# Routed experts in a two-layer decoder: whole rows in the experts' lists, outcomes in rows of their own, and first-layer weights loaded per tile

## The chip, the cores and the metric

The kernel runs on one core of a Trainium2 chip. A core has five engines that run their own instruction streams: TensorE (PE, with its weight loads shown as PEld), VectorE (DVE), ScalarE (ACT), GpSimd (POOL) and SyncE (SP). SP issues the plain DMAs; POOL issues the indirect ones, whose rows are given by a list of indices. The metric is the device time of one execution in microseconds. "Before" is the median of three runs, 733.93 us (733.42 to 735.83).

## The reference, cut to what matters

The reference is a decoder of two layers on x of 4 batches x 256 tokens x 256 channels, with a layer norm after each block. Layer 0 has a sliding-window attention, a cross attention over 1601 context rows and a feed-forward block with ternary weights. Layer 1 has a causal attention with compressed keys, a linear cross attention, and the block that the change is about, a mixture of eight experts of which each token uses two:

```python
logits = 30 * tanh(x @ w_gate / 30)           # x: 1024 tokens x 256
probs = softmax(logits)                       # over 8 experts
_, idx = top_k(probs, 2)
weights = probs * one_hot(idx, 8).sum(-2)
for e in range(8):
    h = silu(x @ w1[e]) * (x @ w3[e])         # 1024 x 512
    out = out + h @ w2[e] * weights[:, e:e+1]
x = layernorm(x + out)
```

All is computed in float32. The kernel computes each expert only for the tokens that chose it.

## The kernel before

**Order of the work.** The kernel's lines do not run in the order in which they stand. A planner, `Loom`, collects every operation with a duration, the tiles that it reads and writes and a priority, and `weave` then emits one at a time: the one that can start first by the planner's own clock, and among equals the one of lowest priority number. Each engine's order is thereby fixed when the program is built. `LAT` and `RATE` are the planner's constants for hops between engines and for DMA; `View` keeps which box of a tile an operation touches, from which the planner finds what depends on what. A `piece` is a group of PE instructions that are planned together.

**The stages.** For each batch of 256 tokens (two row tiles of 128, called t = 0 and t = 1): `l0_attention`, `l0_cross`, `l0_ffn`, `l1_attention`, `l1_cross`, `route`. `ternary` prepares the feed-forward weights of layer 0: it loads three matrices of 1 MB into `raw` (two buffers), sums their magnitudes on DVE, adds the sums over partitions by a small product on PE (`wabs` with `ones`), and loads the matrices again to round them. The stages of different batches overlap as the planner finds room.

**The experts before.** `route(b)` stores the batch's rows to two arrays in DRAM, `xd` (the rows to gather) and `acc` (to which outcomes are added). It computes the gates, each token's two experts and its place in each expert's list, and writes an entry of 8 bytes (gate, token number) into `lists` with four indirect DMAs. `tile_table` turns the counts into a table: for each expert tile of 128 list rows, which expert and which first row. It runs twice: once before the last batch is routed, for the tiles that are sure to be full (`EARLY`, 5), and once after (`LATE`, 18). There are 23 tiles in all, since a list's last tile is padded.

`expert_tile` does one tile. SP reads the first row from the table and fetches the tile's 128 entries; POOL gathers the tokens' rows from `xd` into `xg`; PE transposes them; PE multiplies with w1 and w3 of the expert, the tokens' rows being the stationary side and the weights, 512 wide, the moving one; ACT, DVE make the hidden layer `eh`, tokens on partitions; PE transposes it in four blocks, ACT copies it to `ehT`; PE multiplies with w2; DVE scales by the gate; POOL adds the outcome to `acc` with an indirect DMA that accumulates. The weights of all experts stand in SBUF: `w13` is loaded once layer 0 has freed its place, `w2e` once the even batches' attention buffers are free. The tiles' working buffers (`p6`) open when the last batch's `l1_attention` has ended, as they take its place.

At the end the four batches are loaded from `acc`, normalised and stored.

Of the kernel before, what the change touches and what calls it, by code (L numbers as in the profile page):

```python
# [23 lines left out]
F32 = mybir.dt.float32  # L24
# [22 lines left out]
class View:  # L47


    def __init__(self, buf, box, shape, steps=()):  # L50
        self.buf, self.box, self.shape, self.steps = buf, box, tuple(shape), steps

    def _with(self, name, args, kw, shape, box=None):
        return View(self.buf, box or self.box, shape, self.steps + ((name, args, kw),))

    def __getitem__(self, key):
        keys = key if isinstance(key, tuple) else (key,)
        keys += (slice(None),) * (len(self.shape) - len(keys))
        spans, shape = [], []
        for k, n in zip(keys, self.shape):  # L60
            if isinstance(k, slice):
                lo, hi, _ = k.indices(n)
                spans.append((lo, hi))
                shape.append(hi - lo)
            else:
                spans.append((k, k + 1))
        return self._with("__getitem__", (key,), {}, shape, None if self.steps else tuple(spans))
# [108 lines left out]
class Loom:  # L176
# [12 lines left out]
    RATE = 0.25  # L189
# [22 lines left out]
    def op(self, ways, outs, ins, claims=(), after=(), size=None, land=1.6, what="", unordered=False):  # L212
# [6 lines left out]
        for v in outs:  # L219
            b = v.buf  # L220
            if not unordered:
                op.deps.update(o for box, o in b.writes if meet(box, v.box))
            op.deps.update(o for box, o in b.reads if meet(box, v.box))
# [16 lines left out]
    def piece(self, us, claims=(), ins=(), what=""):  # L240
# [5 lines left out]
        self.op({"PE": (us, us, lambda: [f() for f in fns])}, outs, ins, claims, what=what)  # L246
# [54 lines left out]
    def weave(self):  # L301
# [11 lines left out]
        while left:  # L313
# [22 lines left out]
            if op.size is not None:  # L336
                self.free["DMA"] = max(self.free["DMA"], at + us) + op.size / self.RATE
                op.end, op.engine = self.free["DMA"] + op.land, "DMA"
# [70 lines left out]
def decoder(ctx: ExitStack, tc: tile.TileContext, a: dict, out: bass.AP):  # L409
# [23 lines left out]
    down = scope("left", [even], on=experts)  # L433
# [15 lines left out]
    p6w, p6d = experts.pool("p6w"), down.pool("p6d")  # L449
# [138 lines left out]
    def normalise(x):  # L588
        mv = tiny((P, 2, 2), "mv")
        for t in range(2):  # L590
            st = tiny((P, 6), "st")
            k.vector.bn_stats(st, x[:, t, :])
            k.vector.bn_aggr(mv[:, t, :], st)
        rstd = tiny((P, 2), "rstd")
        k.gpsimd.tensor_scalar(rstd, mv[:, :, 1], 1e-5, None, ALU.add)
        k.gpsimd.tensor_tensor(rstd, rstd, mhalf, ALU.pow)
        for t in range(2):
            k.vector.tensor_scalar(
                x[:, t, :], x[:, t, :], mv[:, t, 0:1], rstd[:, t : t + 1], ALU.subtract, ALU.mult
            )  # L600

    def norm(b, x):

        normalise(x)
        xt = xpool.tile((P, 2, S), F32, "xt")
        ps = bank((P, 2, 2, P))
        for t in range(2):
            with piece(0.22, [xt], what="norm"):
                for c in range(2):
                    turn(ps[:, c, t, :], x[:, t, c * P : (c + 1) * P], ident)  # L610
        evac(xt.rearrange("p c (t q) -> p c t q", t=2), ps)
        X[b], XT[b] = x, xt
# [12 lines left out]
    def project_out(pool, x_new, t, x_old, o, wo, gate=None):  # L625
# [8 lines left out]
        else:  # L634
            k.vector.scalar_tensor_tensor(oT, gate[:, :, t * P : (t + 1) * P], 1.0, pt, ALU.add, ALU.mult)
# [16 lines left out]
    def l0_attention(b):  # L652
# [11 lines left out]
        for i in range(3):  # L664
            pv = bank((P, D))
            with piece(0.86, what="v"):
# [67 lines left out]
    def feature_map(pool, dst, ps, n, width, bufs=2):  # L734

        e = pool.tile((P, 512), F32, "fm", bufs=bufs)[:n, :width]
        k.scalar.activation(e, ps, AF.Exp)
# [314 lines left out]
    def l1_attention(b):  # L1052
# [16 lines left out]
        def four(q4):  # L1069

            ps = project_in(XT[b], lambda c, j: m_w[:, c, 2 * q4 + j, :], [qeT], "q")
            evac(qeT[:, 2 * q4 : 2 * q4 + 2, :], ps)
            aT0 = pool.tile((P, 2, 2, S), F32, "aTa")
            aT1 = pool.tile((P, 2, 2, P), F32, "aTb")
            for t in range(2):
# [4 lines left out]
                with piece(0.65 if t == 0 else 1.15, [at, aT0, aT1], what="scores"):  # L1080
# [15 lines left out]
                for kc in range(t + 1):  # L1096
# [4 lines left out]
                    dst = aT0[:, :, :, t * P : (t + 1) * P] if kc == 0 else aT1  # L1101
                    evac(dst, pt.rearrange("p (u i) q -> p u i q", u=2))

            po = bank((P, 2, S))
# [452 lines left out]
```

## Time and profile before

| what | before |
|---|---|
| median of three runs | 733.93 us (733.42 to 735.83) |
| the profiled execution | 731.26 us |
| its span, first to last instruction | 729.5 us |
| mean granted TensorE clock | 0.979 |
| busy: PE, DVE, ACT, POOL | 92%, 60%, 41%, 22% |
| moved by DMA | 63.39 MB |

The span and all lines of the profile are of that one execution. A line number such as L253 can be that of a helper through which many operations go (L253 is every matmul, L260 every transpose, L382 every operation of DVE, ACT or POOL), so operations are told apart by the names of the tiles that they write and read. A matmul in float32 shows as two records. Matmuls are pipelined: the time from one start to the next tells what one costs, the duration of a record is longer.

### The profile page before, as it was taken

What the parts mean: (1) busy time and instruction counts of PE and PEld (TensorE: products, weight loads), DVE (VectorE), ACT (ScalarE), POOL (GpSimd) and SP (SyncE); (2) the same over time, 40 slices, a digit from 0 to 9 for tenths busy, and PEclk for the clock granted to TensorE, in tenths of its full rate; (3) what the DMA queues carried; (4) which work ended last, traced back from release to release, by engine and by line L of the source; (5) the groups of instructions that cost most, each with busy time, mean ns of one, the idle gap of its engine ahead of it and who ended that gap; (6) DMA issues with size and microseconds to landing.
All of it is one profiled execution on the core that took longest, in us unless ns stands there. A gap on an engine that the chain in (4) does not pass through costs nothing.

```text
span 729.5 us, 11204 instructions
## 1 busy us (share of the span) xinstructions
PE 672.8 (92%) x3920; PEld 490.8 (67%) x3920; DVE 438.5 (60%) x1067; ACT 302.6 (41%) x931; POOL 158.3 (22%) x190
## 2 busy tenths in 40 slices
PE   7999999999999999999899999999977959999970
PEld 5778787678867786767676777777654635665640
DVE  4899886334493535665999877887754513333323
ACT  2868664211232224343467765656611202222210
POOL 3220324022100000000121010303122456522232
PEclk9999999999999999999999999999999989999995
DMA  9901212538632230000203900003601143312214
GB/s 307 341 18 59 92 35 87 173 128 273 219 115 91 91 122 1 1 0 1 53 1 115 347 1 30 1 30 62 199 2 37 30 56 90 59 21 23 23 22 123
DMA packets 51819, 63.39 MB, mean 87 GB/s; under 512 B 7758, under 2 KB 41684, under 8 KB 51764
## 3 DMA queue, kind: packets, MB, share of 16 engines
q1 hardware_dynamic: 46836, 56.63, 23.9%
q0 software_dynamic: 4928, 6.05, 5.3%
q8 instruction: 32, 0.52, 0.3%
q14 instruction: 23, 0.19, 0.1%
HBM read 54.05 MB, written 8.61 MB: 86 GB/s over the span
## 4 chain that ended last, share of the span: by engine, by line
PE 73%; DVE 13%; DMA 5%; ACT 4%; issue 2%; POOL 1%; SPq 0%; POOLq 0%; DVEq 0%; ACTq 0%
PE bank L253 65%; PE bank L260 8%; DVE at L382 3%; ACT at L382 3%; DMA acc<-ey,mine 2%; DVE nm L382 2%; DVE x L382 2%; DVE h L382 1%; DVE as L382 1%; DMA lists<-entry,rowi 1%; DMA xg<-xd,mine 1%; DVE st L382 1%; DMA x<-acc 1%; POOL rstd L382 1%; DMA wqkv<-in_wqkvT 0%
## 5 line engine op out<-in xcount | busy, mean ns | idle before, releaser
L382 ACT ACTIVATE at<-at,nm 128x128 f32<-128x128 f32 (+1 forms) x256 | 106.3, 418 | 23.5 <-DVE nm L382 22.9
L253 PE MATMUL bank<-w,xgT 128*128 x184 | 85.0, 608 | 0.5 <-ACT xgT L382 0.5
L260 PE MATMUL bank<-ident,at 128*128 128x128 f32 (+1 forms) x440 | 60.4, 275 | 1.1 <-DVE at L382 0.4
L253 PEld LDWEIGHTS bank<-w,xgT 128*128 128x128 f32 x184 | 35.0, 197 | 37.1 <-issue 36.0
L260 PEld LDWEIGHTS bank<-ident,at 128*128 128x128 f32 (+1 forms) x440 | 50.7, 141 | 13.0 <-issue 4.8
L382 POOL TENSOR_SCALAR rstd<-mv 128x2 f32<-128x2 f32 x24 | 6.3, 263 | 244.2 <-DVE mv L382 226.1
L253 PE MATMUL bank<-V,aT 128*128 128x256 f32 (+1 forms) x240 | 55.2, 380 | 1.4 <-DVE o L382 1.4
L253 PE MATMUL bank<-KT,qT 128*128 128x512 f32 (+1 forms) x128 | 53.8, 554 | 0.0
L253 PEld LDWEIGHTS bank<-V,aT 128*128 128x128 f32 (+1 forms) x240 | 45.0, 190 | 11.6 <-issue 4.4
L1357 POOL DMA_INDIRECT acc<-ey,mine x23 | 36.1, 1569 | 72.7 <-DVE ey L382 42.1
L253 PE MATMUL bank<-kf,V 128*128 128x256 f32 (+1 forms) x208 | 49.9, 382 | 1.1 <-DVE kf L382 1.1
L382 DVE TENSOR_REDUCE nm<-at 128x4 f32<-128x512 f32 x64 | 50.7, 809 | 0.5
L253 PE MATMUL bank<-wkv,KT 128*128 128x256 f32 (+1 forms) x208 | 49.7, 383 | 0.0
L382 ACT ACTIVATION_READ_ACCUMULATOR at<-at,nm 128x1 f32 x256 | 48.4, 189 | 0.0
L253 PE MATMUL bank<-w2e,ehT 128*128 x184 | 43.9, 385 | 2.9 <-ACT ehT L382 2.8
L382 POOL TENSOR_TENSOR at<-at,rs 128x512 f32<-128x512 f32 (+1 forms) x17 | 20.3, 1191 | 111.0 <-DVE rs L382 70.0
L253 PEld LDWEIGHTS bank<-kf,V 128*128 128x128 f32 (+1 forms) x208 | 38.5, 190 | 7.7 <-DVE kf L382 2.3
L382 ACT COPY aT<-bank 128x512 f32<-128x512 f32 (+2 forms) x57 | 29.1, 540 | 33.3 <-PE bank L260 33.0
L253 PEld LDWEIGHTS bank<-wkv,KT 128*128 128x128 f32 (+1 forms) x208 | 37.7, 186 | 7.5 <-issue 1.9
L253 PEld LDWEIGHTS bank<-w2e,ehT 128*128 128x128 f32 x184 | 34.0, 190 | 12.3 <-ACT ehT L382 4.4
L382 DVE TENSOR_TENSOR at<-at,rs 128x512 f32<-128x512 f32 (+1 forms) x47 | 39.2, 834 | 1.0
L382 ACT ACTIVATE eh<-bank 128x512 f32<-128x512 f32 x23 | 13.7, 597 | 59.4 <-PE bank L253 59.4
(248 smaller groups left out, 1252.0 us busy)
## 6 DMA issues: line engine op xcount, KB each, us to landing
w<-in_w SPq DMA_DIRECT2D x16, 512.0 KB, 9.3
KT<-in_ctxT SPq DMA_DIRECT2D x6, 1024.0 KB, 6.2
V<-in_ctx SPq DMA_DIRECT2D x6, 1024.0 KB, 7.5
w2e<-in_w SPq DMA_DIRECT2D x8, 512.0 KB, 9.4
KT<-in_ctxT SPq DMA_DIRECT2D x6, 577.0 KB, 4.7
V<-in_ctx SPq DMA_DIRECT2D x6, 512.0 KB, 4.1
wq<-in_w1qT SPq DMA_DIRECT2D x8, 256.0 KB, 4.8
wo<-in_w1o SPq DMA_DIRECT2D x8, 256.0 KB, 3.1
```

The costliest lines, as they stand in the source:

```text
L253: lambda: self.nc.tensor.matmul(real(o), real(lhsT), real(rhs), start=real(start), stop=stop, **kw)
L260: fns.append(lambda: self.nc.tensor.transpose(real(o), real(x), real(ident)))
L382: return getattr(engine, method)(*[real(x) for x in args], **{k: real(x) for k, x in kw.items()})
L1357: nc.gpsimd.indirect_dma_start(out=acc.real(), out_offset=bass.IndirectOffsetOnAxis(ap=ids.real(), axis=0), in_=y.real(), in_offset=None, ...
```

## The change

**The lists.** An entry of `lists` becomes the token's whole row, its gate and the place of its outcome: 258 numbers, 1,032 bytes. `l1_cross` writes its result straight into the entry, `route` copies it to the entry of the token's second expert, and the arrays `xd` and `acc` go. `lists` is first filled with zeros (9216 rows, six DMAs).

**A tile.** The tile's table holds the row numbers, so POOL gathers the tile from `lists` in one indirect DMA, gate and place included; SP's fetch goes. The outcome is written, not added, to a row of its own in a new array `yd`: one for each token's first and one for its second expert, and spare rows for padding. Two such writes are declared to have no row in common.

**The products.** w1 and w3 become the stationary side, in blocks of 128 columns, and the tokens' rows the moving side, so that the hidden layer comes out with its channels on partitions; its transposes and their copy go. w1 and w3 are loaded by SP for each tile into one of four buffers `wt`, by the expert's number from the table, in place of `w13`. `w2e` is loaded where `w13` was.

**The last batch.** `l1_attention`, `l1_cross` and `route` of the last batch run in two halves (t = 0, t = 1). There are three tables: 5 tiles before the first half is routed, 2 before the second, 16 after it.

**The end.** Each batch loads two blocks from `yd` and adds them to its rows on DVE (eight loads, eight additions), then normalises and stores.

**The planner.** `RATE` goes from 0.25 to 0.33, indirect DMAs no longer queue behind others in its clock, `View` keeps boxes through chains of slices, and a `piece` can wait for the readers of a tile that its result will overwrite (`over`, used in `l0_attention` for v).

The diff, cut to its core:

```diff
-    RATE = 0.25
+    RATE = 0.33
...
-    down = scope("left", [even], on=experts)
...
-    p6w, p6d = experts.pool("p6w"), down.pool("p6d")
+    p6w = experts.pool("p6w")
...
-            with piece(0.86, what="v"):
+            with piece(0.86, over=[v], what="v"):
...
+        for ts in ((0,), (1,)) if b == B - 1 else ((0, 1),):
+            for q4 in range(4):
+                four(q4, ts)
...
+            norm_into(xn, xt, ts)
+            yield ts, xn, xt
...
-    EARLY = -(-(2 * 3 * S - NE * (P - 1)) // P)
-    LATE = 2 * T // P + NE - 1 - EARLY
+    EARLY = [-(-(2 * n - NE * (P - 1)) // P) for n in (3 * S, T - P)]
+    EARLY[1] -= EARLY[0]
+    TILES = 2 * T // P + NE - 1
+    LATE = TILES - sum(EARLY)
     LISTS = (NE + 1) * T
+    W = D + 2
...
-    lists = in_dram((LISTS, 2), "lists", I32)
-    xd = in_dram((T + P, D), "xd")
-    acc = in_dram((T + P, D), "acc")
+    lists = in_dram((LISTS, W), "lists")
+    yd = in_dram((2 * T + 1 + TILES * P, D), "yd")
...
+        blank = p3.tile((P, FF), F32, "h")[:, :W]
         k.gpsimd.memset(blank, 0.0)
+        for i in range(0, n, 12):
+            dst = lists[i * P : (i + 12) * P, :].rearrange("(n p) w -> p n w", p=P)
+            filled.append(k.dma_start(dst, blank.unsqueeze(1).to_broadcast([P, 12, W]), after=loaded))
...
+    def scatter(dst, row, src, us, land, what, after=(), level=None):
...
+            d = nc.gpsimd.indirect_dma_start(
+                out=dst.real(),
+                out_offset=bass.IndirectOffsetOnAxis(ap=row.real(), axis=0),
+                in_=src.real(),
+                in_offset=None,
+            )
+            tc.declare_no_dep(d.ins, group=what, reason="no two of them have a row in common")
...
-        for d in (xd, acc):
-            k.dma_start(d[b * S : (b + 1) * S, :].rearrange("(t p) d -> p t d", p=P), X[b])
...
+            x = entry[:, t, :, :D]
+            either(
+                (k.gpsimd, "tensor_copy", (x[:, 1], x[:, 0]), {}),
+                (k.vector, "tensor_copy", (x[:, 1], x[:, 0]), {}),
+                (k.scalar, "copy", (x[:, 1], x[:, 0]), {}),
+            )
...
-        def fetch():
-            first_row()
-            nc.sync.dma_start(out=entry.real(), in_=lists.real()[bass.ds(reg["row"], P), :])
...
-                in_=xd.real(),
-                in_offset=bass.IndirectOffsetOnAxis(ap=ids.real(), axis=0),
+                in_=lists.real(),
+                in_offset=bass.IndirectOffsetOnAxis(ap=rowi[:, i : i + 1].real(), axis=0),
...
-                compute_op=ALU.add,
...
+        def weights():
+            expert(nc.sync)
+            for j, w in enumerate(("w1", "w3")):
+                nc.sync.dma_start(
+                    out=wt.real()[:, j],
+                    in_=a[w][bass.ds(reg[nc.sync], 1), :, :].rearrange("o (c p) n -> p (o c) n", p=P),
+                )
...
+        wt = p6w.tile((P, 2, 2, EI), F32, "wt", bufs=4)
+        k.op({"SP": (1.6, 1.6, weights)}, [wt], [tab], size=8e-6 * D * EI, what="weights")
...
+        h = pool.tile((P, EI // P, P), F32, "eh")
+        pa = [bank((P, EI // P, P)), bank((P, EI // P, P))]
+        with piece(3.52, [h], what="tile"):
             for j in range(2):
+                for m in range(EI // P):
+                    for c in range(2):
+                        mm(pa[j][:, m], wt[:, j, c, m * P : (m + 1) * P], xgT[:, c, :], c == 0, c == 1)
...
-        hT = pool.tile((P, 4, P), F32, "ehT")
-        ph = bank((P, 4, P))
-        with piece(0.44, [hT], what="tile"):
-            for c in range(4):
-                turn(ph[:, c, :], h[:, c * P : (c + 1) * P], ident)
-        evac(hT, ph)
...
-        k.op({"POOL": (1.65, 1.65, add_up)}, [acc], [y, ids], size=0.13, what="add up")
+        scatter(yd, slots, y, 1.0, 2.0, "give")
...
-    w13 = p6w.tile((P, NE, 2, 2, EI), F32, "w13")
-    for e in range(NE):
-        k.dma_start(w13[:, e, 0], rows(a["w1"][e]))
-        k.dma_start(w13[:, e, 1], rows(a["w3"][e]))
-    w2 = p6d.tile((P, NE, 4, D), F32, "w2e")
+    w2 = p6w.tile((P, NE, 4, D), F32, "w2e")
...
     for b in range(B):
-        x = new_x()
-        k.dma_start(x, acc[b * S : (b + 1) * S, :].rearrange("(t p) d -> p t d", p=P))
+        x = X[b]
+        for e in range(2):
+            y = p6.tile((P, 2, D), F32, "back", bufs=4)
+            row0 = 1 + e * T + b * S
+            k.dma_start(y, yd[row0 : row0 + S, :].rearrange("(t p) d -> p t d", p=P))
+            k.vector.tensor_tensor(x, x, y, ALU.add)
         normalise(x)
```

## The prediction

> **What bounds the kernel now.** I read the page first: the share of each engine, the slices of the span and the chain of work that ended last.
>
> ```profile
> PE 672.8 (92%) x3920; PEld 490.8 (67%) x3920; DVE 438.5 (60%) x1067; ACT 302.6 (41%) x931; POOL 158.3 (22%) x190
> ...
> PE   7999999999999999999899999999977959999970
> ...
> PEclk9999999999999999999999999999999989999995
> ...
> PE 73%; DVE 13%; DMA 5%; ACT 4%; issue 2%; POOL 1%; SPq 0%; POOLq 0%; DVEq 0%; ACTq 0%
> ```
>
> PE is the bound nearly everywhere. It gives way in slices 29 to 31 (536 to 605 us), where the experts start, and in the last slice. Asked by windows, 536 to 605 holds 51.69 us of PE work in 69 and a clock of 0.90; 605 to 708 holds 101.10 in 103. So two things are worth money: PE work, and those holes. The timeline of PE shows both:
>
> ```profile
> 541.24 0.67 PE L260 MATMUL bank<-ident,x 128*128 128x128 f32 x4 [3.16 <-DVE x L382]
> ...
> 550.67 0.41 PE L260 MATMUL bank<-ident,xg 128*128 128x128 f32 x2 [2.80 <-DMA xg<-xd,mine]
> ...
> 596.45 0.66 PE L260 MATMUL bank<-ident,xg 128*128 128x128 f32 x2 [7.54 <-DMA xg<-xd,mine]
> ...
> 604.00 3.60 PE L253 MATMUL bank<-w,xgT 128*128 x8
> 607.44 0.60 PE L260 MATMUL bank<-ident,eh 128*128 128x128 f32 x4
> 607.87 3.60 PE L253 MATMUL bank<-w,xgT 128*128 x8
> ```
>
> Brackets are idle time and who ended it. All holes of 536 to 605 sum to 17.9 us (0.69, 3.16, 0.67, 2.80, 0.90, 0.35, 0.68, 7.54, 0.46, 0.66). Starts give prices: 8 records of w1/w3 take 3.44 us (0.43 each), four transposes of eh 0.44. A f32 matmul is two records. Why the gather that ends the 7.54 was late is in POOL's timeline:
>
> ```profile
> 583.49 0.96 POOL L1215 DMA_INDIRECT lists<-entry,rowi  x1 [0.30 <-issue]
> 584.75 1.59 POOL L1357 DMA_INDIRECT acc<-ey,mine  x1 [0.30 <-DVE eh L382]
> 591.48 1.56 POOL L1357 DMA_INDIRECT acc<-ey,mine  x1 [5.14 <-DMA acc<-ey,mine]
> 593.34 1.02 POOL L1349 DMA_INDIRECT xg<-xd,mine  x1 [0.31 <-issue]
> ```
>
> An add-up waits until the one before it has landed, and the gathers stand behind it in POOL's order. The end is the same wait, in the chain:
>
> ```profile
> 705.75 3.72 DMA acc<-ey,mine
> ...
> 710.20 3.73 DMA acc<-ey,mine
> ...
> 714.89 4.01 DMA x<-acc
> ```
>
> PE ends at 708.1 and the span at 729.5: a tail of 21.4 us.
>
> [...]four 128x128 records of wkv,gT start at 196.23 and the next group at 196.67, 0.11 each, as fast as transposes; so 128-wide products are no slower per column[...]. [...]after the 3.16 hole the 16 records of wqg take 5.29 us and not 3.72. [...]no run here shows gathers beside a load of weights, so their delay is bounded below. [...]the trace has 5.4 us for scatters of 8-byte entries against 2.8 for gathers of 1 KB rows.
>
> **The change, part by part.** 23 tiles in both kernels.
>
> *Hidden layer transposed by construction.* w1 and w3 become the stationary side, so eh needs no transposes: 92 x 0.109 = -10.0 us. Their products become 23 x 32 = 736 records at 0.112 = 82.4 us for 184 x 0.429 = 78.9: +3.5. Bounds: 0.109 (transposes), giving +1.3, and 0.13 (the 128x136 records of kvs,qf, 512.93 to 513.97), giving +17. I take 0.112, as wkv,gT is the same shape. ACT's copy of ehT (0.59 each) goes too, hidden but for the last ones.
>
> *One gather, no fetch.* The fetch (1.7 us to land, after SP's register loads) leaves the chain from routing to first product. Scatters now carry 1,032 B; bounds of landing 2.6 us (fastest gather) and 6.3 (the slowest 8-byte one of 536 to 545); I take 3.7, that of an add-up of 1 KB rows. From the rank products of batch 2: 1.25 us to the first scatter (533.4 to 534.65), four issues at 1.29, landing 3.7 after the fourth, 0.4, gather 3.0: first xg at +12.2. The changed PE order puts 11.7 us of other pieces in between (wqg, scores, pv, out, priced as above). Stall 0.5, range 0 to 4.
>
> *No wait between outcomes.* Rows of their own let outcomes be written without order. After the last rank products PE has w2 and w1/w3 of remaining early tiles, 12.7 us; two scatters and a gather need 10 to 12. The 7.54, 0.46 and 0.66 go.
>
> *Last batch in halves.* Expert buffers open only after its attention, so early tiles still cannot fill that, but two early tables and the cross half now fill the norms' waits: 3.16 and 2.80 are covered by w1/w3 of tiles 1 and 2 (3.6 each). New holes: the last head group's softmax (mask 1.4, max 1.2, exp 2.0, multiply 1.2, hops: 6.3) has 2.9 of cover, so 3.4; eviction of qeT 0.8; the first tile 0.5; the norm's rstd on POOL queues behind five gathers (6.3 us), PE waits for it about 1; small ones 1. Sum 7 left of 17.9: -10.9. Of the 4.7 us that the slow clock cost there (1.6 wqg, 1.1 and 1.5 w1/w3, 0.5 kvs) half goes: -2.3. The extra routing and table work of DVE (some 8 us) lies beside PE pieces; DVE is busy 26 of 69 there.
>
> *w1 and w3 per tile.* 24 MB through SP, one MB for each 5.5 us of PE, four buffers. The old load of w1/w3 ran at 385 GB/s (windows 400 to 415): 2.7 us per MB. Hidden; without that cover each us over 5.5 is paid per tile.
>
> *Filling the lists.* 9.5 MB in place of 2.4, queued on SP between the FFN weights' loads near 170 us. The old fill ran at 364 to 387 GB/s (windows 177.5 to 187.5): 25 to 30 us. The raw weight behind it lands near 210, its sum (2.3) is done near 213; PE meets the product of these sums near 218, by its order. Hidden with 5 us to spare; stores to xd and acc vanish.
>
> *The end.* ey, issue, landing: +4.2 us after PE (it was +5.8, two add-ups in a row), first load 2.7 later. DVE then has eight additions of 128x512 (0.6) beside the old work of 7.4: 12.4. Then 5.5 as before (724.0 to 729.5): 24.8 against 21.4, +3.4.
>
> *Planner.* RATE 0.33 and finer boxes re-order all stages; I expect nothing, within 3 us, since the early PE order differs only in interleaving.
>
> Sum: -10.0 + 3.5 - 10.9 - 2.3 + 3.4 = -16.3. The profiled execution was 731.26 (span 729.5), so 715.0 for its like; the median of runs is 733.93, 2.7 above it, so 717.6: say 717.5.
>
> **Rivals.** *The holes stay* (0.17): gathers beside 4 MB of weights land late, the first tile and the late tiles wait 5 us each: 727. [...]against: the order leaves 0.7 to 3 us of room. *The plan covers more* (0.12): the clock stays up, the softmax hole closes: 708. *The fill is late* (0.07): [...]PE waits 5: 722.5. *Slower* (0.09): the stream of weights becomes the bound. Each late tile then takes the load's time; it undoes the gain at 16.3 / 16 = 1.0 us more per tile, 6.5 us per MB or 160 GB/s. At 6.9 us: 717.6 + 22 = 740. For it: 512 KB took 9.3 us to land in the page's issues; against: that was the eighth in a queue moving 385 GB/s. That the change doesn't do what it says I give nothing: the transposes are gone from the order.
>
> **Numbers.** Likeliest 0.55: 717.5, own range 712 to 723. Faster: 0.55 + 0.17 + 0.12 + 0.07, less 0.03 for results near no change: 0.88. Within 0.3% (2.2 us, about what a measurement of this kernel can tell from no change): 0.03. Slower 0.09. Range 706 to 730: it leaves out the slower case and the outer parts of the second and third.
>
> **What would show it.** Right: no ident,eh; w1/w3 records 0.11 apart; PE idle under 8 us where 17.9 was; outcomes on POOL with no wait for one another; eight loads and 25 us after PE. Wrong: PE waiting for wt, for xg over 2 us, or for the sums of raw near 218; PE records of xgT,wt over 0.12 apart, which at 0.13 alone gives back 13 us.

## The result, and the profile after

The changed kernel takes 732.53 us (median of 20 runs, 726.92 to 734.21) where the kernel before, in the same comparison, takes 735.10 (median of 20, 732.07 to 738.22). The ratio is 0.9954, with a 95% interval of 0.9935 to 0.9973: half a per cent faster, clear of the noise, where 717.5 us had been forecast. The profiled execution took 726.92 us, its span is 725.2, its mean granted clock 0.971. Four of the 20 runs, the profiled one (the fastest) among them, show a clock of 0.971 or 0.973 and take 726.9 to 729.1 us, the other sixteen 0.966 or 0.967 and 731.7 to 734.2, so the profile shows less than the typical run loses.

The page of the changed kernel first: PE and its granted clock in 40 slices of 18.1 us, and the shares of the chain of work that ended last.

```profile
PE   7999999999999999999899899999988979979960
...
PEclk9999999999999999999999999999999989989995
...
PE 74%; DVE 9%; issue 5%; ACT 5%; POOL 3%; DMA 2%; another core or an unknown queue 1%; SPq 0%; POOLq 0%; DVEq 0%; ACTq 0%
```

PE works 669.5 us in all (672.8 before). The slices 30, 31 and 33, which had stood at 7, 7 and 5, have 8, 8 and 7: the holes are smaller. But slice 36, full before, has 7, and "issue" has grown from 2% to 5% of the chain: time in which the engine waited for nothing that the profile names. Of it, 4.4 us are PE's, near 592, and some 26 are POOL's, between 603 and 641. The timeline of PE shows the holes (start, duration, operation and count; the bracket is the idle time before it and what ended it, "remote" standing for something that the trace does not name):

```profile
406.88 2.79 PE L267 MATMUL bank<-ident,at 128*128 128x128 f32 x12 [2.47 <-ACT at L397]
...
537.58 0.41 PE L267 MATMUL bank<-ident,o 128*128 128x128 f32 x2 [2.66 <-DVE o L397]
...
551.08 0.41 PE L267 MATMUL bank<-ident,xg 128*128 128x128 f32 x2 [1.56 <-remote]
...
585.90 5.52 PE L260 MATMUL bank<-xgT,wt 128*128 128x128 f32 x48
592.14 0.27 PE L260 MATMUL bank<-xgT,wt 128*128 128x128 f32 x1 [0.72 <-issue]
...
598.53 2.28 PE L260 MATMUL bank<-xgT,wt 128*128 128x128 f32 x9 [0.34 <-issue]
600.61 2.17 PE L260 MATMUL bank<-w2e,eh 128*128 x8
...
642.39 0.82 PE L267 MATMUL bank<-ident,xg 128*128 128x128 f32 x6
647.70 3.78 PE L260 MATMUL bank<-w2e,eh 128*128 x8 [4.49 <-DVE eh L397]
```

The products of w1 and w3 are cheap where nothing disturbs them: the 48 records from 585.90 on start 0.112 apart, and no transpose of `eh` is left. There are three new losses. Near 405, in the first batch's `l1_attention`, PE waits 2.47 us for ACT's `at`; the kernel before has no such hole there. Between 591.3 and 598.5 the records that should follow each other at 0.11 come 0.7 or 1.4 us apart; the 64 records from 585.90 would have been issued by 593.1, and the next product starts at 600.61, 7.5 us late. And at 647.70 PE has waited 4.49 us for DVE's `eh`. The trace's record of the granted clock has a drop to half speed with each of them: 3.4 us from 406.6, 6.8 from 594.3 and 6.8 from 645.5. The last begins inside the hole and outlasts it by 4.7 us, in which PE loses 2.3. One more, of 3.4, begins at 539.7, behind the hole of 2.66.

In POOL's timeline the outcomes (`yd`) have indeed lost their wait for one another; six gathers in a row follow them:

```profile
586.82 0.96 POOL L1259 DMA_INDIRECT yd<-ey,slots  x1 [0.30 <-DVE ey L397]
588.09 0.96 POOL L1259 DMA_INDIRECT yd<-ey,slots  x1 [0.30 <-issue]
589.35 0.98 POOL L1410 DMA_INDIRECT xg<-lists,rowi  x1 [0.30 <-DVE rowi L397]
...
595.65 0.95 POOL L1410 DMA_INDIRECT xg<-lists,rowi  x1 [0.30 <-issue]
...
640.25 0.96 POOL L1410 DMA_INDIRECT xg<-lists,rowi  x1 [5.41 <-DVE ey L397]
641.52 0.98 POOL L1259 DMA_INDIRECT yd<-ey,slots  x1 [0.30 <-issue]
```

The last two lines are a gather and a scatter of the steady phase; they come back below. What holds `eh` up at 647 stands in DVE's timeline:

```profile
639.90 0.67 DVE L397 SCALAR_TENSOR_TENSOR eh<-eh,bank 128x512 f32<-128x512 f32 x1
646.69 0.16 DVE L397 SCALAR_TENSOR_TENSOR slots<-xg,spare 128x1 int32<-128x1 f32 x1 [6.12 <-DMA yd<-ey,slots]
646.88 0.16 DVE L397 TENSOR_TENSOR slots<-slots,xg 128x1 int32<-128x1 int32 x1
646.96 0.68 DVE L397 TENSOR_TENSOR eh<-bank,eh 128x512 f32<-128x512 f32 x1
```

The kernel's lines for these operations, in `expert_tile`, cut:

```python
slots = p5.tile((P, 1), I32, "slots", bufs=8)
...
k.vector.scalar_tensor_tensor(slots, slot, 0.0, own_row, ALU.is_equal, ALU.mult)
k.vector.tensor_tensor(slots, slots, slot, ALU.add)
```

The second half of the gated product, 0.68 us of work that PE needs next, stands in DVE's order behind a pair of operations of 0.16 us each. These make the places to which an outcome is written (`slots`), one number per row, for a tile whose turn on PE comes several tiles later. The first of them waits for two transfers by its semaphores: for the gather of its own tile, sent at 640.25 and landed at 643.8, and for the scatter of the tile eight before, which reads the same one of eight buffers; that one was sent at 641.52 and landed at 646.6. The chain that ended last goes through it, and shows the end:

```profile
641.52 5.08 DMA yd<-ey,slots
...
705.26 4.05 DMA back<-yd
```

PE ends at 701.0 and the span at 725.2: a tail of 24.2 us, where 24.8 had been worked out.

### The profile page after: what moved, and what is told of

Read it like the earlier page. It is cut to its first block, busy times and chain, and to the rows that moved or that the text cites. A ratio compares the mean times of both kernels' runs of the same rounds, so it can differ in the third digit from the quotient of the medians.

```text
span 725.2 us, 12255 instructions
## 1 busy us (share of the span) xinstructions
PE 669.5 (92%) x4411; PEld 534.4 (74%) x4411; DVE 445.7 (61%) x1157; ACT 297.0 (41%) x929; POOL 149.5 (21%) x193
## 4 chain that ended last, share of the span: by engine, by line
PE 74%; DVE 9%; issue 5%; ACT 5%; POOL 3%; DMA 2%; another core or an unknown queue 1%; SPq 0%; POOLq 0%; DVEq 0%; ACTq 0%
PE bank L260 65%; PE bank L267 9%; ACT at L397 3%; DVE at L397 3%; DVE nm L397 2%; DMA yd<-ey,slots 1%; POOL xg L1410 1%; DVE entry L397 1%; POOL rstd L397 1%; POOL yd L1259 1%; POOL lists L1259 1%; DMA back<-yd 1%; DVE x L397 0%; DVE st L397 0%
## 5 line engine op out<-in xcount | busy, mean ns | idle before, releaser
L260 PE MATMUL bank<-xgT,wt 128*128 128x128 f32 x736 | 89.1, 279 | 5.4 <-issue 4.4
L260 PEld LDWEIGHTS bank<-xgT,wt 128*128 128x128 f32 x736 | 87.1, 195 | 8.2 <-issue 5.8
L267 PEld LDWEIGHTS bank<-ident,at 128*128 128x128 f32 (+1 forms) x440 | 52.6, 145 | 15.4 <-issue 4.8
L397 POOL TENSOR_SCALAR rstd<-mv 128x2 f32<-128x2 f32 (+1 forms) x26 | 6.9, 264 | 234.2 <-DVE mv L397 202.9
L397 DVE TENSOR_REDUCE nm<-at 128x4 f32<-128x512 f32 (+1 forms) x64 | 50.5, 805 | 0.2
L260 PE MATMUL bank<-w2e,eh 128*128 x184 | 45.7, 394 | 4.5 <-DVE eh L397 4.5
L397 ACT ACTIVATE eh<-bank 128x512 f32<-128x512 f32 x23 | 13.7, 597 | 87.7 <-PE bank L260 57.6
L397 ACT COPY aT<-bank 128x512 f32<-128x512 f32 (+2 forms) x60 | 31.3, 551 | 30.1 <-PE bank L267 29.4
L397 POOL TENSOR_TENSOR at<-at,rs 128x512 f32<-128x512 f32 (+1 forms) x20 | 23.4, 1168 | 95.7 <-DVE rs L397 89.6
L260 PEld LDWEIGHTS bank<-w2e,eh 128*128 128x128 f32 x184 | 34.7, 198 | 8.8 <-DVE eh L397 4.7
L397 ACT ACTIVATE fm<-bank 128x512 f32<-128x512 f32 (+2 forms) x33 | 18.2, 553 | 48.0 <-PE bank L260 48.0
```

What stands on the lines that cost most here:

```text
L260: lambda: self.nc.tensor.matmul(real(o), real(lhsT), real(rhs), start=real(start), stop=stop, **kw)
L267: fns.append(lambda: self.nc.tensor.transpose(real(o), real(x), real(ident)))
L397: return getattr(engine, method)(*[real(x) for x in args], **{k: real(x) for k, x in kw.items()})
```

## The experiments

Two theories for the missing time, A and B, were put on record with the first runs. A: the wait of `slots` on DVE. B: the burst of six gathers makes PE crawl near 592. Times compare within one submission, that is among kernels that ran together; the kernel before ran in each, and ratios are to it. PE's end in a profile is set beside the time, since it leaves the tail out.

**The changed kernel again.** No edit.

> The changed kernel once more, unedited, for a second trace. Theory A (a wait of DVE): the operation that makes an outcome's places waits on DVE for the gather of its tile and for the landing of the scatter eight tiles before, and the gated products of another tile are queued behind it; the order of work is fixed, so the hole of PE of 4.5 us near 647 is there again, between 2 and 6 us. Theory B (a burst): PE's crawl of 592 to 598.5, nine records in 7.4 us, is there again, between 3 and 10 us, since six gathers and eight loads of weights meet at the same place of the order. Rival: both are chance of one execution, and neither is there. Median expected 732.5, between 731 and 734.

725.88 us (720.72 to 726.98), before 731.29: ratio 0.990 (0.9869 to 0.9930). The median lies under the 731 to 734 that were expected. In its profile PE waits for `eh` behind `slots` again (the gather had taken 4.8 us to land and the scatter 5.1), here in PE's and in DVE's timeline:

```profile
646.61 3.78 PE L260 MATMUL bank<-w2e,eh 128*128 x8 [4.72 <-DVE eh L397]
```

```profile
645.60 0.16 DVE L397 SCALAR_TENSOR_TENSOR slots<-xg,spare 128x1 int32<-128x1 f32 x1 [6.15 <-DMA yd<-ey,slots]
```

The drop of 6.8 us in the clock comes with it, from 645.1. So A is part of the kernel. (Two of the six runs took 720.7 us, with a clock of 0.976 and 0.978; what they were spared is not known, as the profile is of another.) The crawl is not there: the records of w1 and w3 run through at 0.112. B is not in every execution, though the order of work is the same.

**More buffers for the places.**

```diff
-        slots = p5.tile((P, 1), I32, "slots", bufs=8)
+        slots = p5.tile((P, 1), I32, "slots", bufs=24)
```

> 24 buffers in place of 8 for the places of the outcomes, so that none of them waits for an earlier scatter; the wait for the own gather stays. In the trace of the changed kernel the scatter that ended the wait near 647 landed at 646.6, the gather at 643.8. Theory A: the hole of 4.5 us shrinks to about 1.7, and the slow clock behind it (3.4 us lost) goes with it: 5 to 7 us less than the changed kernel, about 726.5. Rival (the wait for the gather is the one that counts, the scatter only the later of two): less than 2 us gained.

718.47 us (714.17 to 722.19), 0.9804 (0.9780 to 0.9829): 7.4 less than e1_again. Yet the hole in its profile, which is of its slowest run, shrank to 3.50 us, at 651.15, and not to 1.7. DVE's timeline in it:

```profile
649.54 0.16 DVE L397 SCALAR_TENSOR_TENSOR slots<-xg,spare 128x1 int32<-128x1 f32 x1 [5.55 <-DMA xg<-lists,rowi]
649.61 0.68 DVE L397 SCALAR_TENSOR_TENSOR eh<-eh,bank 128x512 f32<-128x512 f32 x1
```

The scatter is out of it and the gather holds DVE alone. Sent at 644.26, beside a load of weights sent at 644.11, it landed at 649.5, 5.3 us later. The size of the hole is set by a landing time that isn't constant (3.6 us for the gather near 640 in the first profile, 4.8 in e1_again's). The profile does not show where the 7.4 us come from: its PE is 4.4 us ahead of e1_again's at 541, before the experts, and 4.0 at the end.

**The places made late.**

```diff
         k.vector.tensor_tensor(slots, slots, slot, ALU.add)
+        places_ops = k.ops[-2:]
...
         k.vector.tensor_tensor(h, pa[1], h, ALU.mult)
+        for o in places_ops:
+            o.deps.add(k.ops[-1])
```

> The two operations that make a tile's places come on DVE behind the gated product of the same tile (a dependence for the planner), when gather and old scatter have long landed. Theory A: no hole of PE near 647 and no slow clock behind it: 7 to 9 us less than the changed kernel, about 725; the crawl of 592 to 598.5 stays. Rival (PE waits there for the xg of its own tile, or for weights, and DVE is only the last in line): a hole of the same size remains under another name, and no more than 2 us are gained.

718.42 us (715.43 to 719.10), 0.9806 (0.9784 to 0.9828): 7.5 less than e1_again. PE's timeline at the place of the hole:

```profile
640.63 0.82 PE L267 MATMUL bank<-ident,xg 128*128 128x128 f32 x6
641.28 1.89 PE L260 MATMUL bank<-w2e,eh 128*128 x8
643.01 7.31 PE L260 MATMUL bank<-xgT,wt 128*128 128x128 f32 x64
```

No bracket is left, and the clock record has no drop between 560 and the tail. PE ends at 692.2 (e1_again: 700.2). The two profiles stand together until the experts begin (the second half of the last batch's products of `w2o` starts at 545.76 here, at 545.86 there), so the 8.0 us come after that. By the records the hole of e1_again and the slow clock behind it are 4.7 and 2.7. No work was removed: two operations of 0.16 us per tile moved behind the one that they had held up. That is theory A shown. The crawl, which had been expected to stay, is not there either.

**Fewer gathers in a row.** The edit of e3_late, and:

```diff
-        xg = p5.tile((P, W), F32, "xg", bufs=8)
+        xg = p5.tile((P, W), F32, "xg", bufs=4)
```

> As the run before, and 4 buffers in place of 8 for gathered tiles, so that gathers follow one by one and no more than 4 stand in a row. Theory B (a burst of gathers beside the loads of weights stalls PE): the crawl of 592 to 598.5 goes, with its 4.4 us of idle time and 3 to 4 us of slow clock: 7 us less than the run before, about 718. Rival C (the loads of weights alone are late, or PE's own supply of instructions): the crawl stays at 4 to 8 us, and the time is that of the run before within 2 us. A gather that now comes too late for its tile would show as PE idle before xg, over 1 us.

718.99 us (717.25 to 722.88), 0.9845 (0.9820 to 0.9871). There was no crawl to remove in e3_late. By the medians this run costs 0.6 us, by the ratios nearly 3, with a wait of 2.35 for `xg` at 599.68. Of B it says nothing.

**Parts of the change undone, on the base of e3_late.** First the base itself, once more.

> The kernel with the places made late (e3_late), unedited, as the base of the next three on the same chip. It took 0.9806 of the kernel before; expected 0.976 to 0.985 of it here. No hole of PE near 640 to 650.

718.27 us (714.85 to 718.61), 0.9799 (0.9780 to 0.9818). As expected.

The products as before, w1 and w3 moving, `eh` transposed:

```diff
-                for m in range(EI // P):
-                    for c in range(2):
-                        mm(pa[j][:, m], wt[:, j, c, m * P : (m + 1) * P], xgT[:, c, :], c == 0, c == 1)
+                for c in range(2):
+                    mm(pa[j], xgT[:, c, :], wt[:, j, c, :], c == 0, c == 1)
...
+            for c in range(EI // P):
+                turn(pt[:, c, :], hr[:, c * P : (c + 1) * P], ident)
+        evac(h, pt)
```

> On the base of e3_late, the products of w1 and w3 as in the kernel before: w the moving side in 184 records of 128x512, and the hidden layer transposed (92 transposes, a copy to SBUF each). The prediction's working said that the new form saves 10.0 of transposes and pays 3.5 for the shorter records, 6.5 in all: so 6 to 8 us more than e5_late_again. Rival (the new form saves nothing, since PE waits for other things in this phase): within 2 us of it. Rival (the copy and one more hop per tile open new holes): over 10 us more.

731.04 us (725.69 to 737.63), 0.9984 (0.9968 to 0.9999): 12.8 more than e5_late_again, twice the term. By records the term is right: the starts of 8 moving records and 4 transposes take 3.87 us per tile (0.429 and 0.109 each in this profile too), those of the 32 of the new form 3.58, which is 6.7 over 23 tiles. The old form also brings waits, in PE's timeline:

```profile
579.04 0.41 PE L267 MATMUL bank<-ident,entry 128*128 128x128 f32 x2 [2.96 <-DVE entry L397]
...
702.57 1.99 PE L260 MATMUL bank<-w2e,eh 128*128 x8 [0.73 <-ACT eh L397]
```

The copy after the transposes is a hop that a tile's last product can wait for, four times for 0.3 to 0.7 us, 1.9 in all, and one new hole of 2.96 stands before the transposes of `entry`. All holes of PE after 535 sum to 11.9 us, to 8.5 in e5_late_again. That makes some 10 us; another 1.7 of the difference between the two profiles lie before 500, where the edit changes nothing. The time is that of the third expectation, over 10 us more; copies and new holes are a third of it.

The last batch in one piece:

```diff
-        for ts in ((0,), (1,)) if b == B - 1 else ((0, 1),):
+        for ts in ((0, 1),):
...
-    EARLY[1] -= EARLY[0]
+    EARLY[1] = 0
```

> On the base of e3_late, the last batch in one piece, as in the kernel before: one early table, and the tiles of the second one come with the late ones. The prediction's working said that the halves cover two waits (3.2 and 2.8 us) and the slow clock behind them, and pay with the softmax hole (3.4) and small ones: with the halves undone the holes before the first tile return, and the late tiles wait for the last scatters with less early work in between: 4 to 10 us more than e5_late_again. Rival (the single gather and the missing wait of the outcomes do it alone, and the halves cost as much as they cover): within 2 us.

731.55 us (729.41 to 732.28), 0.9996 (0.9986 to 1.0005): 13.3 more. PE's timeline:

```profile
535.03 4.56 PE L260 MATMUL bank<-w2o,qeT 128*128 128x256 f32 x20
553.10 0.66 PE L267 MATMUL bank<-ident,xg 128*128 128x128 f32 x2 [13.50 <-DMA xg<-lists,rowi]
...
600.81 0.66 PE L267 MATMUL bank<-ident,xg 128*128 128x128 f32 x2 [6.34 <-DMA xg<-lists,rowi]
```

Here the whole length of the way from routing to the first tile lies open. Four scatters are sent from 536.40 on, the last lands at 545.9, the gather is sent at 546.68 and lands at 552.96: 16.6 us where the working had 10.9 for the same part of it. The gather alone took 6.3 us, for which 3.0 had been put; four loads of 1 MB were under way beside it. The clock is at half speed for 17.1 us from 542.4 on, of which 6.4 lie behind the hole. The halves cover more than was thought because there is more to cover.

The planner's rate back at its old value:

```diff
-    RATE = 0.33
+    RATE = 0.25
```

> On the base of e3_late, the planner's rate of a transfer back at 0.25. The prediction's working gave the planner's new numbers nothing, within 3 us: the same as e5_late_again within 3 us. Rival (the old rate makes the planner hold work back for transfers that land sooner, and a gain of the change comes from it): 4 us more or over.

723.42 us (719.03 to 725.07), 0.9893 (0.9878 to 0.9909): 5.2 more, so the rival holds. Its profile fell on its fastest run, and there PE ends at 692.0 as in e5_late_again; so it does not show the 5.2 us. It has one new hole, PE waiting 4.86 us for `xg` at 600.12, where e5_late_again has 0.54. The number is a guess about DMA, and by it the planner decides what PE has left to do while the last gathers land.

**The stream of weights.** The changed kernel, with w1 and w3 loaded for the first four tiles only:

```diff
-        wt = p6w.tile((P, 2, 2, EI), F32, "wt", bufs=4)
-        k.op({"SP": (1.6, 1.6, weights)}, [wt], [tab], size=8e-6 * D * EI, what="weights")
+        if len(kept) < 4:
+            wt = p6w.tile((P, 2, 2, EI), F32, "wt", bufs=4)
+            k.op({"SP": (1.6, 1.6, weights)}, [wt], [tab], size=8e-6 * D * EI, what="weights")
+            kept.append(wt)
+        wt = kept[(len(made) - 1) % 4]
```

> The changed kernel with the loads of w1 and w3 of the first four tiles alone; every later tile multiplies with what stands in those four buffers, so its outcome is that of another expert. 4 MB are loaded in place of 23, the rest is as it was, the places still made where they wait. Question: is it the stream of weights that makes gathers and scatters land late (4.8 and 5.1 us near 640 in e1_again, 2.4 to 2.8 where no load runs)? Theory: yes; both land in 2.4 to 2.8 there, the hole of PE near 647 shrinks from 4.7 to about 2, and the slow clock behind it may go: 3 to 7 us less than the changed kernel, 0.981 to 0.986 of the kernel before. Rival (scatters and gathers disturb one another, the stream has no part in it): landings and hole as before, the time within 1.5 us of the changed kernel.

719.58 us (717.84 to 723.76), 0.9795 (0.9764 to 0.9826), where the changed kernel has 0.990 to 0.995 in its three submissions. In its profile the outcomes' landings that the trace holds take 2.39 to 3.17 us, all but one of them under 2.6; with the stream, in e1_again, 2.39 to 6.06. The hole at 647 is not shrunk but gone. The first gathers, beside the four loads that remain, still take 7.0, 6.5 and 6.0. Of the later gathers one has all its records, and took 2.79. So it is the stream that makes gathers and scatters late, scatters by up to 3.7 us. The products it never makes late: in none of these profiles does a wait of PE end with `wt`. The crawl near 592 is there, 3.7 us of idle time in pieces, with no load anywhere near it: the stream is not its cause.

**Fewer buffers for weights, and more for the end,** three edits of one number on the base of e3_late: `wt` with `bufs=2`, with `bufs=3`, and `back` with `bufs=8`. The base did not run beside them, so their times are not set against it.

> On the base of e3_late, two buffers for w1 and w3 of a tile in place of four: all work stays, and only 2 MB can be under way when the first gathers are sent. If the stream delays the gathers, the first ones land in 3 to 4 us and not 6, PE's waits for xg of 1.3 and 1.4 us near 553 go and with them a slow window: 2 to 5 us less than e3_late. Rival (a tile's weights then come too late): a load of 1 MB takes 2.7 us where alone, and a tile of PE 5.3, so the wait for the weights shows as PE idle before xgT,wt over 0.5 us per tile, and the time is higher, 2 to 20 us.

723.95 us (720.72 to 726.94), 0.9853 (0.9817 to 0.9888). The theory missed: with 2 MB ahead of them the first gathers land in 6.5 and 5.9 us, no sooner. PE's waits near 551 are 1.23 for `xg` and 0.69 for its copy. No wait for weights shows, so its rival missed too. PE waits 6.14 us at 603.30 for the copy of a gathered tile, while ACT and DVE stand idle, ACT for 13.8 us and DVE for 9.3, beside a burst of five gathers and more: the crawl in another form.

> As the run before with three buffers, which leaves the order of PE nearly as in e3_late. 3 MB ahead of the first gathers in place of 4: the waits near 553 shrink by about half or not at all, since the first two gathers are sent behind 2 MB in any case: within 2 us of e3_late. No wait for weights.

727.37 us (724.19 to 728.02), 0.9880 (0.9850 to 0.9910).

> On the base of e3_late, eight buffers in place of four for the outcomes that are read back at the end, so that no load there waits for an addition. In e3_late DVE ran from 698.2 to 711.5 of the tail with 2.1 us of holes (0.2, 1.1, 0.3, 0.2, 0.3). If the loads' wait for buffers is what makes them: 1 to 2 us less. Rival (DVE's own 11 us bound the tail, as the prediction had it): within 0.7 us.

724.04 us (723.48 to 729.23), 0.9870 (0.9837 to 0.9903). DVE runs for 13.8 us in this tail and for 13.4 in e3_late's, with holes of the same size (2.4 and 2.1 us in all): its own work bounds the end, the loads' buffers don't.

The profiles of e11 and e12 both show the crawl, at 598 to 605 and at 594 to 601. They can't be held against e3_late, whose profile has none, as that ran in another submission.

**The crawl.** First the base, the gathers in smaller bursts, and the changed kernel, together.

> e3_late once more, as a base for the next two. If PE's crawl near 592 to 604 is there, 0.983 to 0.989 of the kernel before, otherwise 0.978 to 0.982. No hole of PE near 640 to 650 either way.

> Four buffers for gathered tiles, as e4_late_xg4, where gathers come singly or in twos after the last table. Theory (the burst of six gathers is what holds up the other engines): no stretch of PE records 0.7 us apart, though e13_late has one on the same chip, and 3 to 8 us less than it. Rival (the place of the order or the supply of instructions, whatever POOL does): the stretch is there, the time that of e13_late within 2 us. If e13_late shows no such stretch, this run tells nothing of it and takes the time of e13_late within 2 us.

> The changed kernel once more, on the chip of e13_late: 6 to 9 us over it, as e1_again stood to e3_late (725.9 to 718.4), whether the crawl is there or not; a hole of PE of 3.5 to 5 us near 645.

720.22 us, 0.9837 (0.9814 to 0.9860); 722.97, 0.9853 (0.9832 to 0.9874); 729.87, 0.9946 (0.9927 to 0.9965). None of the three profiles has the crawl, so B was not tested; the four gather buffers cost 2.8 us where 2 had been allowed. The changed kernel takes 9.7 us more than the version with late places, a little over what was said, and its hole is 5.01 us, at 652.01. Not all of the 9.7 need come of the places: when the third batch's products of `w2o` start, before any expert, e15_after's profile is already 4.1 us behind e13_late's (502.60 and 498.54). Two waits show in that part, one of which had been named as a rival. PE's timeline in e15_after:

```profile
218.68 0.39 PE L260 MATMUL bank<-wabs,ones 128*128 128x3 f32 x2 [2.63 <-DVE wabs L397]
```

This is the product of the sums of raw, late by 2.63 us (1.56 in e13_late, 1.58 in e14_late_xg4, nothing in the changed kernel's own profile): the filling of the lists, 9.5 MB ahead of the raw weights in SP's queue, is just about covered, and not always. In e15_after the clock drops by half for 3.4 us behind it, from 220.3, and once more from 356.8. The other is the wait of 2.47 us for ACT's `at` near 410, with its drop of 3.4 us in the clock. It stands in all eighteen profiles after the change, that of e8_late_rate included, so the planner's rate is not its cause; what is was not tried.

The profile of e15_after matters for the result. It took 731.95 us at a mean clock of 0.966, as the sixteen typical runs of the changed kernel did (731.7 to 734.2 at 0.966 or 0.967), and it has no crawl. So the typical time can be reached without the crawl, by the late sums and the drops of the clock beside the hole of A. Whether the sixteen were of this kind isn't shown, as none of them was profiled.

Then the base and the smaller bursts once more:

> e3_late again, to see whether this chip shows the crawl of PE near 592 to 604 (6 to 8 us of records 0.7 us apart). With it 0.983 to 0.989 of the kernel before, without it 0.978 to 0.984.

> Four buffers for gathered tiles: after the last table two gathers in a row and then single ones, where e16_late has six in a row. Theory (the burst of gathers holds up the other engines): where e16_late has the crawl this run has none, or one of under 2 us, and takes 2 to 8 us less. Rival (the supply of instructions, or the place in the order): the crawl is there in both. If e16_late has none, nothing is told by this run.

726.53 us (723.85 to 728.36), 0.9882 (0.9835 to 0.9929), and 722.61 (720.00 to 723.72), 0.9833 (0.9788 to 0.9879). This time the base has the crawl. PE's timeline in e16_late, in e13_late and in e17_late_xg4:

```profile
592.70 6.08 PE L260 MATMUL bank<-xgT,wt 128*128 128x128 f32 x53
599.62 0.39 PE L260 MATMUL bank<-xgT,wt 128*128 128x128 f32 x2 [0.84 <-issue]
...
606.53 3.62 PE L260 MATMUL bank<-w2e,eh 128*128 x8
```

```profile
592.16 7.31 PE L260 MATMUL bank<-xgT,wt 128*128 128x128 f32 x64
599.30 1.89 PE L260 MATMUL bank<-w2e,eh 128*128 x8
```

```profile
599.47 0.38 PE L267 MATMUL bank<-ident,xg 128*128 128x128 f32 x2
602.35 0.41 PE L267 MATMUL bank<-ident,xg 128*128 128x128 f32 x2 [2.50 <-DMA xg<-lists,rowi]
```

From the first of the 64 records to the next product it is 7.1 us in e13_late and 13.8 in e16_late. POOL sends the six gathers from 596.15 to 603.4 there; the crawl begins two gathers into the burst and ends two microseconds after it, and ACT (10.3 us idle until "remote") stands still with PE. With four buffers two gathers come in a row and then single ones, and no record is held up; PE pays 2.50 us for a gather that now comes later. PE ends at 701.3, 692.3 and 695.7. The medians lie 3.9 us apart, with no run of the one inside the range of the other. This speaks for B, on one profile of each kind: where the base crawls, the smaller bursts do not. But a burst is not enough: e1 to e3, e5 to e8, e13 and e15 have six gathers or more in a row and run through them.

**What stays open** is the condition. In every profile with the crawl (the changed kernel's, e9, e11, e12, e16) and in the two others of their submissions (e10, e17) the trace also holds fewer records of completed transfers: 2,815 to 2,936 (e9, which loads less, 2,484) where the profiles of e1 to e8 and e13 to e15 hold 3,504 to 3,508. That one cause in the recording both loses the records and holds up the engines, so that the crawl would be a loss of the recording and not of the kernel, is the author's guess. Against it, the records go missing long before: between 460 and 480, where the first four scatters land, the changed kernel's profile holds 38 of them and e1_again's 64, and no engine is held up there. In e17 they are missing without any crawl. No run here was timed without a record of its clock, so this is not shown.

Another rival is the supply of instructions. In each of the five profiles with the crawl a load of instructions (16 KB) starts 0.4 to 1.8 us before it (590.1 in the changed kernel's, 597.0 in e16_late). It stands at the same place of the order in e13_late, at 596.5, where nothing follows it, so by itself it is not the cause either; but the smaller bursts move it too (599.4 in e17_late_xg4), so it is not excluded. The share of the crawl in the typical time of the changed kernel is open as well.

**A version that beats both.** e3_late's edit alone gives 0.980 to 0.988 of the kernel before in its four submissions, and with four gather buffers 0.983 to 0.985 in three. Where the changed kernel ran beside them, they take 7 to 10 us less.

## Why the prediction was wrong, step by step

The direction held, the size didn't: 717.5 was forecast, with 706 to 730 as the range, and the median is 732.5. In terms of PE's end, the sum had put it 19.7 us earlier than before, at 688.4; the profile has 701.0, 12.6 later. The three new losses more than cover it: 4.5 us at 647 with 2.3 behind it by the slow clock, 7.5 near 592, and 2.5 near 405 with 1.6 by the clock, 18.4 in all, against which 5.8 were gained elsewhere. Without the first two, in e3_late and e13_late, PE ends at 692.2 and 692.3. The typical run takes 5.6 us more than the profiled one; e15_after's profile suggests where, and no run shows it.

*Hidden layer transposed by construction:* right in its records. 0.112 was taken and 0.112 measured; no transposes of `eh`. Undone, it costs 12.8 and not 6.5: the copy behind the transposes, called hidden, shows 1.9 us of waits, and a hole of 2.96 comes with the changed order.

*One gather, no fetch:* the sizes were wrong and the sum nearly right. Scatters of 1,032 B land in 2.5 to 5.2 us (3.7 was taken), but the first gathers, beside the loads, in 5.6 to 5.9 in e1_again (3.0 was taken). The first tile's wait is 1.1 and 1.3 us there, where 0.5 stood, inside its range of 0 to 4. For gathers beside a load of weights the prediction had no run, and bounded the delay from below only. e1_again gives the size, 4.7 to 6.3 us to land beside loads and 2.7 without, and in e9_no_stream a later gather takes 2.79; why the loads delay the gathers is not shown.

*No wait between outcomes:* this is the step that failed, by 7.5 us of the 15. It said that outcomes can be written without order and that 7.54, 0.46 and 0.66 go. They do; POOL's part is right. But the step took the declared freedom of the rows for freedom of the buffers. The change computes each outcome's places on DVE from a gathered tile, into eight buffers, and thereby adds a wait for a gather and one for the scatter eight tiles back, to an engine with `eh` in its queue. For POOL the prediction had named what stands behind a waiting instruction ("the gathers stand behind it in POOL's order"); for DVE it did not ask. The pair of operations, 0.3 us of DVE work per tile, stands in no term of its own; at most it is part of "the extra routing and table work of DVE", taken as work beside PE and never as a wait. In place of none the runs show a hole of PE of 4.5, 4.7 and 5.0 us in the three profiles of the changed kernel, and 7.5 us of time with the slow clock behind it (e3_late against e1_again). With this one wait gone the kernel stands at 0.980 to 0.984 of the kernel before in the three submissions without a crawl, where the forecast was 0.978. That it comes so near is in part luck, as other terms were off by several us in both directions. The rival *the holes stay* had the cause, late gathers, and the wrong place: it looked for the wait in front of `xg` on PE.

*Last batch in halves:* right in its sum. 7 us of holes were forecast for 536 to 605; e1_again has 7.1. The softmax's 3.4 came as 2.66 and 0.72, the first of them as a wait for `o`, which stands behind the softmax's operations on DVE. The profile of the changed kernel has 6.6, and 4.4 of the crawl on top, which nothing in the prediction provided for.

*The slow clock:* half of 4.7 was to remain. In the profile the clock is at half speed for 17.1 us between 480 and PE's end (13.7 before). The hole of 4.49 comes with a drop of 6.8 us, as that of 4.72 in e1_again does, so the missed hole costs 6.8, 4.5 itself and 2.3 by the clock. With shorter ones it varies: the holes of 2.66 and 2.47 come with a drop of 3.4 us each, that of 2.50 in e17_late_xg4 with none.

*w1 and w3 per tile:* the weights are never late, right. Their cover was looked for in the wrong unit: the stream fits in time, but beside it single gathers land in 4.7 and 4.8 us in place of 2.7, and scatters in up to 6.1 in place of 2.4 (e1_again).

*Filling the lists:* no wait in the profile (the product comes at 214.96), with 1.6, 1.6 and 2.6 us in three later ones: the 5 us to spare are not there. The rival *the fill is late* was right in kind, for one of the submissions.

*The end:* 24.2 to 24.7 measured in the three profiles of the changed kernel, 24.8 forecast. *Planner:* nothing was given to it, within 3 us. The third batch's products of w2o start 0.4 us later than before in the profile, 2.6 in e1_again and 7.9 in e15_after. Of this the hole near 405 with its slow clock is 4.0, in every profile; the rate's own part, a gain of 5.2, was undervalued.

## What to carry to other kernels

An operation of 0.16 us that reads a transfer's result is a wait, and costs what stands behind it in its engine's order (here 4.5 to 5.0 us of PE): place it after the work that must not be late, and check how many tiles back its buffer was last read. A declaration that transfers need no order frees the transfers, not the small buffers that feed them. And a stream that keeps its own consumer fed can still lengthen the landing of small gathers and scatters beside it (here from 2.7 to 4.8 us and from 2.4 to 5.1); so price those with the stream running.

## What the runs showed of the hardware that was not expected

In e1_again single gathers of 128 rows of 1,032 B landed 4.7 and 4.8 us after their issue where loads of weights were sent within a microsecond of them, those in a burst beside the loads in up to 6.3, and in 2.7 where no load had been sent in the five microseconds before. Scatters of 1 KB rows went from 2.4 to 6.1. Plain writes of such rows landed in 2.4 us at the fastest (e1_again, e9_no_stream), where the last two adds in the chain of the kernel before had taken 3.72 and 3.73.

Outside the tail, the drops of the granted clock to half speed last 3.41, 3.41 and 6.83 us in the profile of the kernel before (from 542.4, 552.6 and 593.6) and 3.41, 3.41, 6.83 and 6.83 in that of the changed kernel (from 406.6, 539.7, 594.3 and 645.5). In the tails they last 18.5 and 23.7. Those from 406.6 and 539.7 come with holes of PE of 2.47 and 2.66 us, which end at 406.9 and 537.6.

In some executions PE, ACT, DVE and SP are held up together for about 7 us while POOL sends six indirect DMAs in a row, and in others, with the same order of work, not at all (e1_again, e13_late). In the changed kernel's profile, at 590 to 601, PE's next product comes 7.5 us late, ACT is idle for 8.2 us and DVE for 7.3 before they go on, and SP's register operations, of 0.04 us at 599 to 601, take 0.70. Why is open.
